# Two token groups loaded ahead of the factors, a new order of steps, and bias additions by half rows

## The chip, the cores and the metric

The kernel runs on one core of a Trainium2 chip. A core has five engines that run their own instruction streams in order: PE (TensorE, matmuls into the eight PSUM banks), DVE (VectorE), ACT (ScalarE), POOL (GpSimd) and SP (SyncE, which here issues nearly all DMAs). They wait for one another by semaphores. The metric is the device time of one launch in microseconds.

## The reference

There are 8 batches of 1024 tokens with 1024 columns, all float32, and a context of 64 rows per batch with a mask. Cut to what matters:

```python
x = x + xattn(layernorm(x), ctx, mask)       # softmax(scores / 32) times ctx, masked
h = layernorm(x)
mixed = einsum('btd,rde->bte', h, factors)   # 8 factors of 1024 x 1024, summed over r
x = x + mixed / sqrt(8) + bias
```

The sum over r can be taken first, so the second part is one product with the sum of the eight factors, scaled by 1/sqrt(8).

## The kernel before, in words

**Tiling.** The 8192 tokens are cut into 16 groups of 512. A group has four row tiles of 128 tokens, tile t = 2h + q. Two groups share one context ("memory").

**One group.** Its tokens are loaded twice: as rows (`load_rows`, L304) and, for groups from 2 on, in blocks (`load_blocks`, L293) that DVE transposes (`transpose_blocks`, L349). Groups 0 and 1 are transposed on PE (`transpose_x_pe`, L375). Then come `scores`, `scores_back`, `softmax`, `weights_back`, `read_out` (PE) and `residual` (DVE, L468, adds the attention into the rows). The first layer norm's statistics come from DVE (`row_stats`, group 0) or ACT (`row_sums`, `row_squares`). The second norm's statistics come from DVE for q = 0 (`norm_stats`, L478) and from ACT for q = 1 (`norm_sums`, `norm_squares`, L497 and L507), each followed by a few small POOL operations. `normalize` (ACT, L523) writes h. From group 1 on, h is moved by 16 DMAs of 64 KB (`relayout`, L546) and transposed by DVE (`transpose_rows`, L555); group 0 does this on PE (`transpose_h_pe`).

**The product.** h times the summed factors is done by a scheme with seven products in place of eight, for each q (`product g q p`, L585, 8 matmul instructions each). Its operand sums are made by `combine_rows` on DVE (L567). Three of the seven (p = 2, 3, 4, the list `SECOND`, L192) are split once more into seven `part g p i` (L634, 4 matmul instructions), which take both q at once, with `combine_parts` (L609). So a group has 8 `product` steps and 21 `part` steps. `give` (L601) and `give_part` (L650) add a product from PSUM, scaled, into the rows x; several products share a bank, so the next one into the bank waits for the `give` of the one before it. `add_bias` (POOL, L538) adds the bias to one row tile. `store` (L665) writes a row tile out.

**The factors.** A piece `load_factor s r` (L670) is a quarter s of the contraction of factor r, 1 MB. s = 0 and 1 fill b11 and t2, s = 2 and 3 fill b21 and b22 (named as they are held; t1, t3 and t4 are differences of these). A piece is added on DVE (`add_factor`, L676, two additions of 128x1024) or on PE through an identity matmul (`sum_factor`, L694, 8 matmul instructions). `add_sums` (L709) joins both and makes the differences; `combine_factors` (L725) makes those for the parts. `product` 1 and 5 need s = 0 and 1 alone; `product` 6 and 7 need all four quarters.

**What sets the order.** Nothing is scheduled at run time. A hand-held table `START` (L24) is run once, then `LOOP` (L76) is run for g = 0 to 16 with p = g - 1, n = g + 1, m = g + 2; a step that was already done is skipped. The order of the steps is the order of the instructions on every engine and every DMA queue. Buffers are handed out first in, first out (`Slots`, L153): 8 PSUM banks, 11 row tiles x, and 8 buffers of 8 KB per partition ("big") that factors, memory, xT, xb, h, hb and hT share. So a load waits for whatever step gave its buffer back, and everything behind it on SP's queue waits too.

Of the kernel before, what the change touches and what calls it, by code (L numbers as in the profile page):

```python
# [10 lines left out]
F32 = mybir.dt.float32  # L11
BF16 = mybir.dt.bfloat16
AF = mybir.ActivationFunctionType
ALU = mybir.AluOpType
# [10 lines left out]
load_memory 0; load_factor 0 6; add_factor 0 6; centre_memory 0; load_rows 0 0; load_bias;  # L25
constants; load_factor 0 4; load_rows 0 3; load_rows 0 2; add_factor 0 4; load_rows 0 1;
load_factor 0 7; row_stats 0 0; transpose_x_pe 0 1; load_factor 1 2; row_stats 0 1;
transpose_memory 0; load_factor 0 0; transpose_x_pe 0 0; scores 0; masks; scores_back 0;
row_stats 0 2; add_factor 1 2; row_stats 0 3; add_factor 0 0; load_factor 0 5; load_factor 0 3;
load_factor 1 0; softmax 0; load_factor 1 5; sum_factor 0 5; load_factor 2 7; weights_back 0;  # L30
read_out 0 0 0; load_factor 0 2; add_factor 1 5; load_factor 2 6; add_factor 1 0; sum_factor 0 3;
read_out 0 0 1; residual 0 0 1; residual 0 0 0; load_factor 0 1; sum_factor 0 7; add_factor 0 2;
load_factor 2 4; read_out 0 1 1; norm_stats 0 0 0; sum_factor 0 1; load_rows 1 1; add_factor 2 6;
load_rows 1 0; norm_stats 0 0 1; add_factor 2 4; normalize 0 0 0; add_sums 0 1; residual 0 1 1;
normalize 0 0 1; load_factor 1 7; load_factor 2 3; load_factor 2 5; load_factor 1 4;
transpose_h_pe 0 0 0; sum_factor 2 7; add_factor 1 7; load_factor 1 3; transpose_x_pe 1 0;
load_factor 1 6; add_sums 0 0; transpose_h_pe 0 0 1; read_out 0 1 0; add_factor 2 3;
add_bias 0 0 1; sum_factor 2 5; load_rows 1 3; load_factor 1 1; residual 0 1 0; norm_stats 0 1 0;
sum_factor 1 4; sum_factor 1 1; load_factor 2 1; load_rows 1 2; combine_rows 0 0 1;
sum_factor 2 1; norm_stats 0 1 1; add_factor 1 3; load_factor 2 2; add_factor 1 6;  # L40
load_factor 2 0; add_sums 1 1; row_sums 1 0; load_factor 3 0; add_sums 1 0; transpose_x_pe 1 1;
add_factor 2 2; add_factor 2 0; add_bias_v 0 0 0; add_sums 2 1; row_squares 1 0; load_factor 3 4;
add_factor 3 4; scores 1; add_factor 3 0; add_sums 2 0; product 0 0 1; load_factor 3 2;
normalize 0 1 0; normalize 0 1 1; transpose_h_pe 0 1 0; load_factor 3 3; add_factor 3 3;
row_sums 1 1; load_factor 3 1; load_factor 3 6; combine_rows 0 0 2; load_factor 3 7;
transpose_h_pe 0 1 1; product 0 0 5; row_squares 1 1; combine_rows 0 0 3; load_factor 3 5;
add_factor 3 2; sum_factor 3 1; combine_rows 0 0 4; scores_back 1; sum_factor 3 6; give 0 0 1;
load_rows 2 1; load_rows 2 0; add_factor 3 7; combine_rows 0 1 1; sum_factor 3 5; softmax 1;
add_sums 3 1; row_sums 2 0; product 0 1 1; weights_back 1; product 0 0 6; add_sums 3 0;
read_out 1 0 0; combine_parts 0 4 1; combine_factors 4; residual 1 0 0; read_out 1 0 1;  # L50
combine_rows 0 1 2; part 0 4 2; give 0 0 6; part 0 4 1; give_part 0 4 1; combine_parts 0 4 2;
# [54 lines left out]
def kernel(  # L106
# [17 lines left out]
    nc = tc.nc  # L124
# [28 lines left out]
    class Slots:  # L153
# [45 lines left out]
        2: ("a12", "b21", "z", True, ((0, 0),)),  # L199
        4: ("a22", "t4", "u", False, ((1, 0),)),  # L200
    }
    LAST = {"u": 7 if 4 in SECOND else 4, "v": 5 if 3 in SECOND else 3, "z": 2}
    PARTS = {
        1: ("a11", "u", True, (0, 0)),
        5: ("s1", "v", True, (1, 1)),
# [580 lines left out]
```

## Time and profile before

| what | value |
|---|---|
| time, median of 3 runs | 981.09 us (979.46 to 981.38) |
| time of the profiled execution | 981.39 us |
| its span, first to last instruction | 979.6 us |
| busy: PE | 941.1 us (96%) |
| busy: DVE | 838.6 us (86%) |
| busy: ACT | 380.8 us (39%) |
| busy: POOL | 237.9 us (24%) |
| mean granted PE clock | 0.996 |
| moved by DMA | 167.01 MB |

"Busy" is the time in which at least one instruction of the engine runs, and PE's matmuls overlap, so a PE that is 96% busy need not run at its best rate: the starts of neighbouring steps tell more. In the views, a row of the order of time has its start, its length, engine, line, operation, output and input tiles, shapes and count, and in brackets how long the engine was idle before it and what released it. "SPq" rows are DMA issues, so their length is the issuing and not the transfer.

### The profile page before, as it was taken

How to read it: one execution, taken by the hardware profiler on the slowest of the kernel's cores; microseconds unless marked ns; L12 is line 12 of the kernel's file. 1: busy time of each engine (PE TensorE's matmuls, PEld its weight loads, DVE VectorE, ACT ScalarE, POOL GpSimd, SP SyncE). 2: the span in 40 equal slices, each digit the busy share in tenths (PEclk: the TensorE clock that was granted, in tenths of full speed). 3: DMA queues.
4: the chain of work that ended last, by engine and by line, in shares of the span. 5: the costliest groups of instructions: out<-in, count | busy, mean ns of one | idle time of the engine just before them, and what ended most of it. 6: DMA issues, size and time to landing. Idle time of an engine off the chain costs nothing.

```text
span 979.6 us, 11017 instructions
## 1 busy us (share of the span) xinstructions
PE 941.1 (96%) x3456; PEld 547.0 (56%) x3456; DVE 838.6 (86%) x1510; ACT 380.8 (39%) x712; POOL 237.9 (24%) x298
## 2 busy tenths in 40 slices
PE   3889999999999999999999999999999999999998
PEld 2345455655656565655656565564656565565656
DVE  3689999979799887989799697989889788989955
ACT  3035252443616253442623455351714445252300
POOL 0021124312312232411322142321223123132300
PEclk9999999999999999999999999999999999999999
DMA  9999637475565667366465756557474746542412
GB/s 353 418 421 369 179 107 159 126 177 145 158 156 155 151 194 149 109 168 165 153 162 155 164 144 148 140 162 176 151 177 134 172 123 170 142 151 79 100 70 86
DMA packets 93530, 167.01 MB, mean 170 GB/s; under 512 B 12320, under 2 KB 71840, under 8 KB 89376
## 3 DMA queue, kind: packets, MB, share of 16 engines
q1 hardware_dynamic: 93024, 165.20, 58.4%
q10 hardware_dynamic: 448, 1.11, 0.4%
q8 instruction: 27, 0.44, 0.2%
q14 instruction: 31, 0.25, 0.1%
HBM read 101.25 MB, written 33.55 MB: 138 GB/s over the span
## 4 chain that ended last, share of the span: by engine, by line
PE 60%; DVE 26%; DMA 5%; SPq 4%; issue 3%; ACT 1%; POOL 0%; DVEq 0%; ACTq 0%; POOLq 0%
PE yu L592 24%; PE yv L592 7%; PE ro L465 5%; PE y4u L641 4%; SPq L551 4%; PE y3u L641 4%; DVE xT L356 4%; DVE x L655 3%; DVE x L605 3%; DVE hT L560 3%; PE scT L399 3%; DMA f<-in_L_ffn_factors_dram 3%; DVE hT L627 3%; PE y2u L641 2%; PE y4v L641 2%
## 5 line engine op out<-in xcount | busy, mean ns | idle before, releaser
L534 ACT ACTIVATE h<-x,nb,rstd 128x512 f32<-128x512 f32 x128 | 96.2, 822 | 211.6 <-DVE x L473 134.2
L540 POOL TENSOR_TENSOR x<-x,bias_bc 128x1024 f32<-128x1024 f32 x63 | 150.1, 2384 | 73.5 <-DVE x L605 37.7
L592 PE MATMUL yu<-b,hT 128*128 128x512 f32 x256 | 118.0, 604 | 0.0
L592 PE MATMUL yu<-t,s 128*128 128x512 f32 x256 | 115.3, 593 | 0.1
L592 PE MATMUL yv<-t,s 128*128 128x512 f32 x256 | 115.2, 593 | 0.0
L592 PE MATMUL yu<-t,hT 128*128 128x512 f32 x256 | 115.1, 592 | 0.0
L605 DVE SCALAR_TENSOR_TENSOR x<-yu,x 128x512 f32<-128x512 f32 x128 | 82.9, 675 | 19.1 <-PE yu L592 19.1
L473 DVE SCALAR_TENSOR_TENSOR x<-ro,rden,x 128x512 f32<-128x512 f32 x128 | 88.4, 741 | 3.5 <-PE ro L465 3.5
L316 ACT ACTIVATE junk<-x 128x1024 bf16<-128x1024 f32 x60 | 63.2, 1054 | 56.6 <-DMA x<-in_x_dram 55.7
L356 DVE STREAM_TRANSPOSE xT<-xb 128x256 f32<-128x256 f32 x224 | 81.6, 410 | 0.0
L592 PEld LDWEIGHTS yu<-b,hT 128*128 128x128 f32 x256 | 46.3, 189 | 62.6 <-issue 51.8
L592 PEld LDWEIGHTS yu<-t,hT 128*128 128x128 f32 x256 | 48.6, 190 | 54.4 <-issue 50.5
L592 PEld LDWEIGHTS yu<-t,s 128*128 128x128 f32 x256 | 48.4, 190 | 48.7 <-issue 45.7
L592 PEld LDWEIGHTS yv<-t,s 128*128 128x128 f32 x256 | 48.5, 190 | 48.2 <-issue 45.9
L399 PE MATMUL scT<-xT,memT 128*64 128x256 f32 x512 | 66.5, 385 | 9.2 <-DVE xT L356 9.2
L560 DVE STREAM_TRANSPOSE hT<-hb 128x1024 f32<-128x1024 f32 x60 | 73.5, 1227 | 0.7 <-issue 0.6
L328 ACT ACTIVATE junk<-x,nmean 128x1024 bf16<-128x1024 f32 x60 | 68.9, 1149 | 2.9 <-POOL nmean L317 0.7
L490 POOL TENSOR_SCALAR rstd<-mv 128x2 f32<-128x2 f32 x17 | 4.6, 269 | 253.6 <-DVE mv L487 253.6
L465 PE MATMUL ro<-mem,eT 64*128 64x512 f32 x256 | 64.5, 617 | 0.6 <-ACT eT L454 0.6
L655 DVE SCALAR_TENSOR_TENSOR x<-y3u,x 128x256 f32<-128x256 f32 x64 | 26.2, 409 | 43.9 <-PE y3u L641 43.6
L502 ACT ACTIVATE junkz<-x 128x1024 bf16<-128x1024 f32 x30 | 31.7, 1056 | 72.7 <-DVE x L473 72.2
L399 PEld LDWEIGHTS scT<-xT,memT 128*64 128x64 f32 x512 | 37.3, 136 | 36.0 <-DVE xT L356 15.0
(133 smaller groups left out, 1544.2 us busy)
## 6 DMA issues: line engine op xcount, KB each, us to landing
f<-in_L_ffn_factors_dram SPq DMA_DIRECT2D x32, 1024.0 KB, 10.8
x<-in_x_dram SPq DMA_DIRECT2D x64, 512.0 KB, 4.5
out_dram<-x SPq DMA_DIRECT2D x64, 512.0 KB, 4.4
hb<-h SPq DMA_DIRECT2D x480, 64.0 KB, 2.0
xb<-in_x_dram SPq DMA_DIRECT2D x112, 256.0 KB, 6.9
mem<-in_ctx_dram SPq DMA_DIRECT2D x14, 256.0 KB, 3.8
mem<-in_ctx_dram ACTq DMA_DIRECT2D x2, 256.0 KB, 5.8
bias_bc<-in_L_ffn_bias_dram ACTq DMA_DIRECT2D x1, 512.0 KB, 7.9
```

Source lines behind the costliest of these rows:

```text
L316: nc.scalar.activation(junk, st["x", g, t], AF.Copy, accum_out=s1[:, t : t + 1])
L328: nc.scalar.activation(junk, st["x", g, t], AF.Square, bias=nmean[:, t : t + 1], accum_out=ss[:, t : t + 1])
L356: nc.vector.transpose(xT[:, 2 * e + c].rearrange("p (t j) -> p t j", j=Q), xb.rearrange("p t (k e i c) -> p e c t k i", e=NC // 2, i=2, c= ...
L399: nc.tensor.matmul(ps[ts(h, M), : 2 * P], mT[:, c, :], st["xT", g, h][:, c, :], start=(c == 0), stop=(c == NC - 1),)
L465: nc.tensor.matmul(ps, eT[ts(h, M), q, :], m[ts(h, M), ts(n, H)], start=True, stop=True)
L473: nc.vector.scalar_tensor_tensor(xt, st.pop(("ro", g, q, n, h)), rden[:, k : k + 1], xt, ALU.mult, ALU.add)
L534: nc.scalar.activation(to, fr, AF.Identity, bias=nb[:, h : h + 1], scale=rstd[:, h : h + 1])
L540: nc.gpsimd.tensor_add(xt, xt, bias_bc)
L560: nc.vector.transpose(st["hT", g, q][:, h].rearrange("p c (t j) -> p t c j", j=Q), hb[:, h].rearrange("p t (c i) -> p t c i", i=Q),)
L592: nc.tensor.matmul(ps, lhs[:, c, :], wq[right][:, c, :], start=(first and c == 0), stop=(c == KH - 1), skip_group_check=True,)
L605: nc.vector.scalar_tensor_tensor(xt, st["y", g, q, key], ISR, xt, ALU.mult, ALU.add)
L641: nc.tensor.matmul(ps, lhs[:, c, :], wp[p][i][:, c, :], start=(first and c == 0), stop=(c == 1), skip_group_check=True,)
```

## The change

**Both tables are new.** In `START` the row tiles of groups 0 and 1 are loaded first, with only a few factor pieces between them; before, group 1's rows came after 15 to 25 pieces. Pieces are loaded by halves of the contraction: nearly all of s = 0 and 1 ahead of s = 2, and s = 3 last; before, s = 0, 1 and 2 were mixed. Group 1's attention and residual move up, in between the factor sums of s = 0 and 1. `load_bias` moves from the head of the table to behind the factor sums. One piece moves from `sum_factor` to `add_factor` (12 and 20 steps before, 11 and 21 after). `START` ends earlier in group 1: its `product` steps now begin in `LOOP`, which starts just behind `scores` of the group after next.

**Norm statistics.** `norm_stats` (DVE) is in neither table any more; all 32 row tile pairs use `norm_sums` and `norm_squares` (ACT).

**Bias.** `add_bias g q k` now adds half a row tile, k = 2h + n: 128 POOL operations of 128x512 where 63 of 128x1024 on POOL and one on DVE were.

**Loads in the loop.** Before, the four `load_rows m` stood together behind all stores of group p. Now `load_rows m 1` stands behind `store p 3`, `m 0` behind `store p 1`, `m 3` and `m 2` behind `store p 0` and `store g 2`, each ahead of a `relayout`.

**Lists.** `PRODUCTS`, `LAST` and the tag of s1 get cases for 7 and 5 in `SECOND`, and `give_part` runs over the list of places; `SECOND` itself stays (2, 3, 4).

The diff, with the tables cut to the places that the prediction names:

```diff
 START = """
-load_memory 0; load_factor 0 6; add_factor 0 6; centre_memory 0; load_rows 0 0; load_bias;
-constants; load_factor 0 4; load_rows 0 3; load_rows 0 2; add_factor 0 4; load_rows 0 1;
...
+load_memory 0; load_rows 0 2; load_rows 0 0; constants; load_rows 0 1; row_stats 0 0;
+load_rows 1 1; centre_memory 0; load_rows 0 3; load_rows 1 0; row_stats 0 1; masks;
+load_factor 1 0; load_rows 1 2; transpose_memory 0; load_factor 1 3; load_factor 1 1;
...
+load_factor 3 2; add_sums 2 0; combine_parts 0 4 1; sum_factor 3 2; load_factor 3 7; part 0 4 1;
+add_factor 3 3; load_factor 3 0; combine_parts 0 4 2; load_factor 3 5; load_factor 3 4;
+norm_squares 1 0; combine_parts 0 4 3; give 0 0 1; add_factor 3 7; load_factor 3 1;
+load_memory 2; give_part 0 4 1; sum_factor 3 6; normalize 1 0 0; load_blocks 2 0;
+normalize 1 0 1; combine_rows 0 0 4; sum_factor 3 5; give 0 1 1; add_factor 3 0; centre_memory 2;
+add_factor 3 4; add_factor 3 1; load_rows 2 0; add_sums 3 1; product 0 1 5; product 0 0 6;
...
 LOOP = """
...
-transpose_blocks m 1 3; scores m; product n 0 1; scores_back m; combine_rows n 0 1; part g 3 7;
...
+give p 1 7; transpose_rows g 0 1; give_part p 2 7; give_part p 3 6; product g 0 1; part p 3 7;
...
+transpose_rows g 1 0; combine_rows g 0 2; row_squares n 1; part p 3 4; softmax n; product g 0 6;
...
+norm_sums n 0; norm_squares n 0; load_blocks m 1; load_rows m 1; combine_parts g 4 1; part p 3 2;
...
+part g 4 2; give_part g 4 1; part g 4 6; residual n 1 0; store p 1; normalize n 0 0;
+combine_parts g 4 3; give g 1 6; part g 4 5; combine_rows g 1 3; transpose_blocks m 0 2;
+transpose_blocks m 0 3; add_bias g 0 2; combine_rows g 1 4; combine_parts g 2 1; add_bias g 1 0;
+part g 2 1; end_rows p 0; give_part g 4 2; add_bias g 0 0; give_part g 4 6; give_part g 2 1;
+product g 0 7; part g 4 7; normalize n 0 1; combine_parts g 4 4; norm_sums n 1; give_part g 4 5;
...
+combine_parts g 3 1; relayout n 0; part g 3 1; norm_squares n 1; centre_memory m; store p 0;
...
+row_sums m 0; store g 2; product g 1 7; part g 2 7; transpose_blocks m 1 3; load_rows m 3;
+scores m; give_part g 2 2; add_bias g 0 1; combine_parts g 3 4; add_bias n 1 2; part g 3 6;
+load_rows m 2; transpose_rows n 0 0; relayout n 1; part g 3 5;
 """
...
-        6: ("s2", "t2", "u", False, ((0, 1),)),
+        6: ("s2", "t2", "u", False, ((0, 1), (1, 1), (1, 0)) if 7 in SECOND else ((0, 1),)),
...
-    LAST = {"u": 7 if 4 in SECOND else 4, "v": 5 if 3 in SECOND else 3, "z": 2}
+    LAST = {"u": 6 if 7 in SECOND else 7 if 4 in SECOND else 4, "v": 5 if 3 in SECOND else 3, "z": 2}
...
-    def add_bias(g: int, q: int, h: int):
-        xt = st["x", g, 2 * h + q]
-        nc.gpsimd.tensor_add(xt, xt, bias_bc)
-
-    def add_bias_v(g: int, q: int, h: int):
-        xt = st["x", g, 2 * h + q]
-        nc.vector.tensor_add(xt, xt, bias_bc)
+    def add_bias(g: int, q: int, k: int, eng=nc.gpsimd):
+
+        xt = st["x", g, 2 * (k // 2) + q][:, ts(k % 2, H)]
+        eng.tensor_add(xt, xt, bias_bc[:, ts(k % 2, H)])
+
+    def add_bias_v(g: int, q: int, k: int):
+        add_bias(g, q, k, nc.vector)
...
-            ops["s1"] = work.tile([P, KH, P], F32, tag="s1", name=f"s1_{g}_{q}")
+            ops["s1"] = work.tile([P, KH, P], F32, tag=f"s1{q if 5 in SECOND else ''}", name=f"s1_{g}_{q}")
...
-        h, n = PRODUCTS[p][4][0]
         q, k = PARTS[i][3]
-        xt = st["x", g, 2 * h + q][:, 2 * n * HH + k * HH : 2 * n * HH + (k + 1) * HH]
-        nc.vector.scalar_tensor_tensor(
-            xt, st["yp", g, p, key][:, :HH], ISR, xt, ALU.mult, ALU.add
-        )
+        for h, n in PRODUCTS[p][4]:
+            xt = st["x", g, 2 * h + q][:, ts(2 * n + k, HH)]
+            nc.vector.scalar_tensor_tensor(
+                xt, st["yp", g, p, key][:, :HH], ISR, xt, ALU.mult, ALU.add
+            )
```

## The prediction

> **What bounds the kernel.** I read the page's slices first, then the busy time by window, then the order of time on TensorE (PE), and last the waits. The windows (busy us of each engine in each stretch, granted PE clock, DMA share, GB/s):
>
> ```profile
> core 0: us, PE busy (x) PEld busy (x) DVE busy (x) ACT busy (x) POOL busy (x), PEclk, DMA share, GB/s
> 0.00:25.00 25.00, 8.59 (x54) 7.62 (x56) 9.43 (x17) 8.66 (x13) 2.19 (x10) 1.00 0.93 353
> 25.00:50.00 25.00, 20.64 (x67) 8.70 (x64) 17.23 (x23) 3.21 (x12) 1.36 (x4) 0.93 1.01 420
> 50.00:75.00 25.00, 22.31 (x72) 11.05 (x72) 21.24 (x27) 8.60 (x15) 6.77 (x6) 0.93 1.02 421
> 75.00:100.00 25.00, 25.00 (x108) 13.39 (x106) 24.38 (x27) 14.54 (x25) 3.54 (x5) 1.00 0.93 368
> ```
>
> For 100 us the DMA engines are full: 38.8 MB (32 factor pieces, eight token tiles, memory, mask, bias) must come in. PE has gaps only here. PE in order of time, at the marks I use below:
>
> ```profile
> 16.41 3.65 PE L371 MATMUL tp<-ident,x 128*128 128x128 f32 x16 [16.41 <-DMA x<-in_x_dram]
> ...
> 100.56 3.70 PE L704 MATMUL sum<-f,ident 128*128 128x512 f32 x8 [0.40 <-DMA f<-in_L_ffn_factors_dram]
> ...
> 107.75 3.60 PE L592 MATMUL yu<-t,s 128*128 128x512 f32 x8
> ...
> 149.17 3.60 PE L592 MATMUL yu<-b,hT 128*128 128x512 f32 x8
> ```
>
> The last factor piece lands at 100.56; 107.75 is `product 0 0 6`, the first that needs all pieces; 149.17 is `product 1 0 1`. From there PE works back to back to 975.5 (826.3 us), except at the scores:
>
> ```profile
> 199.05 3.67 PE L399 MATMUL scT<-xT,memT 128*64 128x256 f32 x32
> 202.65 3.70 PE L592 MATMUL yu<-b,hT 128*128 128x512 f32 x8
> ...
> 309.40 2.37 PE L399 MATMUL scT<-xT,memT 128*64 128x256 f32 x18
> 312.57 1.94 PE L399 MATMUL scT<-xT,memT 128*64 128x256 f32 x14 [0.80 <-DVE xT L356]
> 314.44 3.70 PE L592 MATMUL yu<-b,hT 128*128 128x512 f32 x8
> ```
>
> Undisturbed scores take 3.60 us from start to the next product; with VectorE (DVE) late they take 5.04. That 1.4 us recurs in 12 groups. `product g 0 1` comes every 55.8 us (149.17 to 874.19, 13 groups); without the wait, 54.4. So a start that is limited by loads and DVE, then a PE-bound loop with one DVE wait.
>
> **Start: what the new order is worth.** PE work ahead of `product 1 0 1`, in back-to-back starts: 96 transposes 11.3, three scores 10.8, twelve `sum_factor` at 3.43 = 41.2, eight products at 3.43 = 27.5, sixteen parts at 0.86 = 13.8, eight `read_out` 7.7, small transposes 2.1: 114.4 us; the other 34.8 of 149.2 are gaps and slow matmuls. The new table puts the same set ahead of `product 1 0 1`, less one `sum_factor` (that piece goes to `add_factor` on DVE, 2.3 us there): 111.0.
>
> Loads: 8.65 MB had moved by 24.5 us and then 420 GB/s, so transfers count from 3.9 us. The three token tiles and the memory (2.1 MB) are in at about 10 us, so PE starts 6 us earlier; that alone is no gain, since PE waits for factors later. Bias (0.5 MB) leaves the load stretch; 38.3 MB end at 96 us if no buffer is late. Two are: `load_factor 3 4` takes the slot of `sum_factor 3 2` (about 90.5) and `load_factor 3 1` that of `add_factor 3 7` (about 92), so the last piece lands at 97 to 98.
>
> What decides is DVE. From `combine_rows 0 1 1` (about 77.4, after the h transposes) to `t2` ready it has five adds at 2.3 = 11.5, `add_sums` 3.7+2.5+2.5 = 8.7, gives and `give_part` 2.7, six combines 2.3: 25.2, so 102.6. I take 104.5 for `product 0 0 6`, 3.2 earlier, with both token groups' attention, `product` 1 and 5 of both row tiles and a part already done. Behind it before `product 1 0 1` stand 4 products, 15 parts, scores and a memory transpose: 13.7+13.0+3.6+0.6 = 30.9 (before: 41.4 elapsed). DVE has 22.6 us of work there until `transpose_blocks 2 1 3` against 22.9 of PE, so it gives no reserve; twelve half bias additions now run here and I charge 2.5 us for collisions. So `product 1 0 1` at 138: **gain 11**, ends 6 (DVE 2 late at 104.5 and 3 late after) and 14 (102.6 and no collision).
>
> **Loop: parts.** `norm_stats` (four BATCH_NORM_STATS2 at 680 ns and two aggregates at 209: in the queue 2.9 us a group) leaves DVE; `norm_sums` and `norm_squares` add 2.33+2.52 us to ACT, 39% busy, whose new chain for q=0 is residual, 2.3, POOL 0.3, 2.5, POOL 1.3, normalize 3.0; with the relayout behind it (10.3 of issues and 1.6) it ends some 4 us before `transpose_rows n 0 0` is due on DVE. Without that reserve, PE would wait by what is missing. Bias: 63 rows of 2384 ns become 128 halves. In proportion a half costs 1.19. [...] POOL is 24% busy; I charge nothing for its own time. What counts is the next view (order of time on POOL and DVE in one group):
>
> ```profile
> 408.76 2.46 POOL L540 TENSOR_TENSOR x<-x,bias_bc 128x1024 f32<-128x1024 f32 x1
> ...
> 408.93 2.58 DVE L627 TENSOR_TENSOR hT<-hT,hT 128x256 f32<-128x256 f32 x1
> ```
>
> The DVE row is normally 0.41; it ended with POOL's. [...] Four such hits a group cost 7.1 us here (L582 1.5, L627 2.2, L631 1.7, L431 1.7). By the row, halves cut each hit; [...] the new table puts three (`add_bias g 0 2`, `g 1 0`, `g 0 0`) in a row right where DVE is tight. That speaks against the change.
>
> **Loop: the new tight place.** With `product g 0 6` as 0, PE needs 20.6 us to the end of `part g 4 1`; `give_part g 4 1` ends at 21.1. It releases `add_bias g 0 2`, then the other two halves. PE wants `part g 4 7` at 27.6, after `give_part g 4 6`: DVE has 5.85 us ahead of it, so 26.95, reserve 0.6. In these 5.85 are four combines that the halves can block: S = 1.3 if DVE goes first, 2.6 [...]. PE's period is then 54.4 + (S - 0.6). The tile scores no longer wait: they come 8 us of DVE work later than needed.
>
> A second cycle closes over SP. The loads of tokens are now each behind a store whose row buffer they take, and `relayout n 1` is behind them:
>
> ```profile
> 471.71 0.34 SPq L666 DMA_DIRECT2D out_dram<-x  x1
> 472.10 3.03 SPq L306 DMA_DIRECT2D x<-in_x_dram  x3
> 480.35 10.54 SPq L551 DMA_DIRECT2D hb<-h  x16
> ```
>
> The third load there waited until the store landed, 3.1 us after its start; sixteen relayout issues take 10.3. New cycle: 21.1, DVE to `give_part g 4 4` 14.9 + S, store 3.1, load issue 0.5, relayout 10.3, landing 1.6, `transpose_rows g 1 0` 1.2, `combine_rows g 0 2` 0.7, hand-overs 0.2: 53.6 + S, back at `product g 0 6`. Queued behind that DVE transpose are softmax and all gives, behind the product the rest of PE. Both cycles give 55.1 to 56.5 for S from 1.3 to 2.6. I take 55.5, nearer to DVE going first, [...]: 0.27 x 13 = **gain 3.5**.
>
> **No cost.** The lists for 5 and 7 in `SECOND`, the tag of s1 and the loop in `give_part` make the same instructions with `SECOND = (2, 3, 4)`. The end keeps its form: last `give_part`, store, 4.1 us.
>
> **Sum.** 979.6 - 11 - 3.5 = 965.1 span; outside it lie 1.8 us (981.39 - 979.6), so **967 us**; the profiled run is 0.3 above the median shown.
>
> **Rivals.**
> 1. *Forecast*, 0.47: own range 957 to 976 (start 6 to 14, period 55.1 to 56.0).
> 2. *Dense loop*, 0.2: halves hardly collide, S under 0.6, period 54.4: 13 x 1.37 = 17.8 with the start, 952.6. For it: DVE loses 2.9 us a group and half a lock. Against: three halves in a row.
> 3. *SP's queue becomes the bound*, 0.15: the store lands in 4.4, as the page's median, or S is 3 or more; period 57.5, 13 x 1.7 = 22.5 lost, minus 11: 993. It decides from a period of 56.6 (0.85 x 13 = 11). For it: every load waits for a store just ahead of sixteen issues. Against: 3.1 measured with a load right behind.
> 4. *The start gives nothing*, 0.18: slot waits starve the loads or DVE is 8 us late, `product 1 0 1` at 147: 976, to 981 if the loop is as before.
>
> Within 0.2% (2 us, about what this kernel's measurement can tell) lie parts of 3 and 4: 0.06. Slower: most of 3, 0.14. Faster: 0.8. The range 950 to 984 leaves out the far end of 3 and a little below 2.
>
> **What would show it.** Start: `product 0 0 6` at 103 to 106, `product 1 0 1` at 135 to 141, its factor wait gone from PE. Loop: no wait of scT for xT; a PE gap ahead of y4u (`part g 4 7`) or ahead of `product g 0 6`, released by DVE; combines above 0.41 us beside half bias rows of 1.2 to 1.3. Wrong if `product 1 0 1` comes after 143, or if the period is under 55.0 or over 56.6.

## The result, and the profile after

The changed kernel takes **970.75 us** (median of 4, 968.06 to 973.52) where the kernel before takes 981.16 in the same comparison: ratio 0.9898, 95% interval 0.9865 to 0.993. Six more executions, taken later beside the experiments, have a median of 968.67 (966.97 to 976.93). The profiled execution took 971.97, with a span of 969.7.

First the windows of the changed kernel over the stretch that was shown of the kernel before (busy us of each engine, granted PE clock, DMA share, GB/s), with the window behind it:

```profile
0.00:25.00 25.00, 13.91 (x83) 11.39 (x84) 10.12 (x21) 12.24 (x25) 2.19 (x10) 0.94 0.95 357
25.00:50.00 25.00, 22.48 (x103) 11.72 (x101) 17.42 (x23) 18.78 (x41) 6.94 (x7) 0.93 0.91 372
50.00:75.00 25.00, 22.84 (x72) 10.98 (x73) 24.41 (x30) 18.12 (x32) 6.60 (x9) 1.00 0.99 394
75.00:100.00 25.00, 25.00 (x68) 11.93 (x67) 23.36 (x28) 6.48 (x10) 2.85 (x4) 1.00 0.98 384
100.00:125.00 25.00, 20.81 (x63) 11.17 (x63) 21.39 (x32) 5.47 (x9) 3.02 (x4) 0.93 0.89 187
```

PE does 5.3 us more in the first window than before and starts at 8.03 in place of 16.41. But the loads run at 372 and 394 GB/s where they ran at 420 and 421, so less had come in by 75 us. What this does to PE's marks stands in its order of time:

```profile
104.54 1.88 PE L588 MATMUL yu<-t,s 128*128 128x512 f32 x4
110.61 3.62 PE L588 MATMUL yu<-t,s 128*128 128x512 f32 x4 [4.19 <-DVE t L716]
...
134.37 3.67 PE L395 MATMUL scT<-xT,memT 128*64 128x256 f32 x32
...
141.63 1.13 PE L637 MATMUL y3u<-b,r 128*128 128x256 f32 x4 [0.80 <-DVE x L651]
142.60 1.03 PE L637 MATMUL y2u<-tau,hT 128*128 128x256 f32 x4
143.47 2.74 PE L588 MATMUL yu<-b,hT 128*128 128x512 f32 x6
```

`product 0 0 6` begins at 104.54 with its first half of the contraction and stands 4.19 us for t2 before the second half. `product 1 0 1` comes at 143.47, against 149.17: the start gives **5.7 us**. From there to the end it is 969.7 - 143.47 = 826.2 us against 830.4: the loop gives **4.2**. In the loop, scores no longer wait, and one gap stands in their place (PE's order of time, two stretches):

```profile
303.44 3.67 PE L395 MATMUL scT<-xT,memT 128*64 128x256 f32 x32
307.04 1.13 PE L637 MATMUL y3u<-b,r 128*128 128x256 f32 x4
...
399.48 3.60 PE L588 MATMUL yu<-t,hT 128*128 128x512 f32 x8
404.04 1.13 PE L637 MATMUL y4u<-tau,hT 128*128 128x256 f32 x4 [0.96 <-DVE x L651]
```

The second gap is the one at `part g 4 7` and comes in every group. It is the only wait of PE that the view of waits shows between the scores at 192.32 and those at 859.07 (us in total, times, longest):

```profile
PE y4u L637 <- DVE x L651: 11.5, 12, 1.0
```

These scores are 12 groups apart, so the period is **55.56 us**; by the same measure the kernel before has 55.84. DVE in the same place, then POOL (order of time):

```profile
396.23 0.42 DVE L651 SCALAR_TENSOR_TENSOR x<-y4u,x 128x256 f32<-128x256 f32 x1 [4.05 <-PE y4u L637]
...
398.82 1.18 DVE L574 TENSOR_TENSOR hT<-hT 128x512 f32<-128x512 f32 x1
...
401.83 1.49 DVE L617 TENSOR_TENSOR r<-hT 128x256 f32<-128x256 f32 x1
...
403.57 0.41 DVE L651 SCALAR_TENSOR_TENSOR x<-y4u,x 128x256 f32<-128x256 f32 x1
```

```profile
396.73 4.39 POOL L537 TENSOR_TENSOR x<-x,bias_bc 128x512 f32<-128x512 f32 x3 [1.60 <-DVE x L651]
401.10 0.21 POOL L500 TENSOR_SCALAR zm<-zs 128x2 f32<-128x2 f32 x1
401.27 1.76 POOL L537 TENSOR_TENSOR x<-x,bias_bc 128x512 f32<-128x512 f32 x1
```

The first DVE row is `give_part g 4 1`, the last `give_part g 4 6`. Between them two combines are long: L574 by 0.5 us (normally 0.68) and L617 by 1.08 (normally 0.41). Their sum is the prediction's S, here 1.58. The first lies beside the three halves that the prediction named. The longer one lies beside a **fourth** half, at 401.27: `add_bias n 0 3`, which stands further down in the table, and which POOL reaches this early because it waits for nothing there. So DVE and POOL hold each other up: the combine takes 1.49 in place of 0.41, and the half beside it 1.76, where the one at 393.86, with DVE idle, takes 1.28. This is called the lock from here on.

### The profile page after: what moved, and what is told of

Its sections match the earlier page's. It is cut to its first block, busy times and chain, and to the rows that moved or that the text cites. A ratio compares the mean times of both kernels' runs of the same rounds, so it can differ in the third digit from the quotient of the medians.

```text
span 969.7 us, 11176 instructions
## 1 busy us (share of the span) xinstructions
PE 930.3 (96%) x3448; PEld 548.4 (57%) x3448; DVE 734.7 (76%) x1409; ACT 462.4 (48%) x848; POOL 280.3 (29%) x363
## 4 chain that ended last, share of the span: by engine, by line
PE 71%; DVE 19%; DMA 6%; issue 1%; ACT 1%; POOL 1%; SPq 1%; DVEq 0%
PE yu L588 26%; PE yv L588 10%; PE y3u L637 6%; PE scT L395 5%; DVE x L469 5%; PE y4u L637 5%; PE y2u L637 4%; DMA out_dram<-x 3%; PE y3v L637 3%; PE y2v L637 3%; DMA f<-in_L_ffn_factors_dram 2%; DVE xT L352 2%; DVE r L617 2%; PE ro L461 2%; DVE x L651 2%; PE y3z L637 2%
## 5 line engine op out<-in xcount | busy, mean ns | idle before, releaser
L537 POOL TENSOR_TENSOR x<-x,bias_bc 128x512 f32<-128x512 f32 x128 | 187.6, 1482 | 84.0 <-DVE x L651 70.3
L588 PE MATMUL yu<-b,hT 128*128 128x512 f32 x256 | 114.9, 592 | 0.0
L498 ACT ACTIVATE junkz<-x 128x1024 bf16<-128x1024 f32 x64 | 67.6, 1057 | 66.3 <-DVE x L469 65.3
L509 ACT ACTIVATE junky<-x,zm 128x1024 bf16<-128x1024 f32 x64 | 73.6, 1149 | 28.5 <-POOL zm L500 27.4
L500 POOL TENSOR_SCALAR zm<-zs 128x2 f32<-128x2 f32 x32 | 11.1, 348 | 259.5 <-ACT junkz L498 259.5
L556 DVE STREAM_TRANSPOSE hT<-hb 128x1024 f32<-128x1024 f32 x60 | 74.0, 1233 | 10.3 <-DMA hb<-h 10.3
L588 PEld LDWEIGHTS yu<-b,hT 128*128 128x128 f32 x256 | 48.6, 190 | 54.8 <-issue 54.0
L651 DVE SCALAR_TENSOR_TENSOR x<-y4u,x 128x256 f32<-128x256 f32 x64 | 26.5, 415 | 63.2 <-PE y4u L637 63.2
L461 PE MATMUL ro<-mem,eT 64*128 64x512 f32 x256 | 62.0, 613 | 0.8 <-ACT eT L450 0.6
L313 POOL TENSOR_SCALAR nmean<-sum 128x2 f32<-128x2 f32 x30 | 10.9, 362 | 178.9 <-ACT junk L312 178.9
```

What stands on the lines that cost most here:

```text
L461: nc.tensor.matmul(ps, eT[ts(h, M), q, :], m[ts(h, M), ts(n, H)], start=True, stop=True)
L498: nc.scalar.activation(junk, st["x", g, 2 * h + q], AF.Copy, accum_out=s1[:, h : h + 1])
L509: nc.scalar.activation(junk, st["x", g, 2 * h + q], AF.Square, bias=nmean[:, h : h + 1], accum_out=ss[:, h : h + 1])
L537: eng.tensor_add(xt, xt, bias_bc[:, ts(k % 2, H)])
L556: nc.vector.transpose(st["hT", g, q][:, h].rearrange("p c (t j) -> p t c j", j=Q), hb[:, h].rearrange("p t (c i) -> p t c i", i=Q),)
L588: nc.tensor.matmul(ps, lhs[:, c, :], wq[right][:, c, :], start=(first and c == 0), stop=(c == KH - 1), skip_group_check=True,)
```

## The experiments

Each was compared with the kernel before on its own chip, and its median stands here with the ratio to that and the 95% interval. "Period" is from the scores of the profiled execution, 12 groups apart; "t2" is the start of the second half of `product 0 0 6`, "p101" that of `product 1 0 1`. These three come from one profiled execution each, which in three kernels (the same again; fourth half later; two factor additions with the fourth half later) is the slowest of its own.

| kernel | median, us | ratio to before | period | t2 | p101 |
|---|---|---|---|---|---|
| changed kernel | 970.75 | 0.9898 (0.9865 to 0.993) | 55.56 | 110.61 | 143.47 |
| the same again | 968.67 | 0.9888 (0.9861 to 0.9915) | 55.56 | 107.47 | 147.01 |
| fourth half later | 955.54 | 0.9755 (0.9726 to 0.9784) | 54.48 | 107.26 | 145.07 |
| three halves later | 957.28 | 0.9772 (0.9744 to 0.98) | 54.49 | 108.32 | 140.47 |
| all four later | 958.65 | 0.9777 (0.9753 to 0.9801) | 54.34 | 105.85 | 143.51 |
| whole bias rows in LOOP | 975.08 | 0.9951 (0.9935 to 0.9967) | 55.94 | 106.92 | 141.59 |
| norm_stats back on DVE | 975.24 | 0.9945 (0.9928 to 0.9961) | 55.56 | 108.25 | 147.75 |
| new START, old LOOP | 978.60 | 0.9978 (0.996 to 0.9995) | 55.92 | 106.11 | 138.36 |
| softmax gap filled | 973.19 | 0.993 (0.991 to 0.995) | 55.56 | 110.64 | 143.48 |
| four later, gap filled, b22 first | 959.82 | 0.9799 (0.9775 to 0.9822) | 54.34 | 109.34 | 143.25 |
| two factor additions earlier | 972.65 | 0.9904 (0.9869 to 0.9939) | 55.56 | 105.98 | 143.71 |
| the same, and fourth half later | 951.93 | 0.9713 (0.9697 to 0.9729) | 54.48 | 107.63 | 140.70 |
| the same, and START's halves moved | 956.95 | 0.977 (0.9749 to 0.9791) | 54.48 | 106.17 | 142.64 |

### The loop: which half makes the gap

The fourth half moved alone:

```diff
-transpose_blocks m 1 0; give_part g 2 6; part g 2 2; add_bias n 0 3; end_rows p 1; give g 0 7;
+transpose_blocks m 1 0; give_part g 2 6; part g 2 2; end_rows p 1; give g 0 7;
...
-scores m; give_part g 2 2; add_bias g 0 1; combine_parts g 3 4; add_bias n 1 2; part g 3 6;
+scores m; give_part g 2 2; add_bias g 0 1; add_bias n 0 3; combine_parts g 3 4; add_bias n 1 2;
```

> Only `add_bias n 0 3` moves in LOOP, from behind `part g 2 2` to behind `add_bias g 0 1`. In the changed kernel this half ran from 401.27 to 403.03 in the group looked at, and `combine_parts g 2 1` stood from 401.83 to 403.32 beside it, some 1.08 us over its 0.41; PE's gap ahead of `part g 4 7` was 0.95. Theory A (the fourth half, which the prediction did not count, makes the gap): the combine falls back to 0.4, the gap goes, the period goes from 55.56 to 54.5 to 54.8 (12 to 13 groups by 0.8 to 1.05), time 957 to 962. Theory B (the three halves of the prediction make it): the combine loses its stall only to the third of the three or to the hand-over, the gap stays at 0.7 or more, period 55.3 to 55.6, time 968 to 972.

The three halves moved alone, and below it all four moved:

```diff
-transpose_blocks m 0 3; add_bias g 0 2; combine_rows g 1 4; combine_parts g 2 1; add_bias g 1 0;
-part g 2 1; end_rows p 0; give_part g 4 2; add_bias g 0 0; give_part g 4 6; give_part g 2 1;
+transpose_blocks m 0 3; combine_rows g 1 4; combine_parts g 2 1; part g 2 1; end_rows p 0;
+give_part g 4 2; give_part g 4 6; give_part g 2 1;
...
-give_part g 4 3; transpose_blocks m 1 1;
+give_part g 4 3; add_bias g 0 2; add_bias g 1 0; add_bias g 0 0; transpose_blocks m 1 1;
```

> Only the three halves `add_bias g 0 2`, `g 1 0`, `g 0 0` move behind `give_part g 4 3`; `add_bias n 0 3` stays. Moving the fourth half alone has already closed PE's gap at `part g 4 7`. Theory A (the three push the fourth into the place: they hold POOL from 396.7 to 401.1, and the fourth waits behind them and the small POOL operation zm): without them the fourth runs at about 399.9 to 401.2, ahead of `combine_rows g 1 4` at 401.26, the combines have no stall above 0.2, the gap is below 0.3, the period 54.4 to 54.7, time 955 to 960. Rival (the fourth is enough by itself: it starts when zm and ACT's normalize let it, which is late in any case): a combine is still stalled by 0.8 to 1.1, the gap is 0.4 to 0.7, the period 54.8 to 55.2, time 962 to 967.

> The three halves `add_bias g 0 2`, `g 1 0`, `g 0 0` move behind `give_part g 4 3`, and `add_bias n 0 3` behind `add_bias g 0 1`; nothing of POOL's bias work is then between `give_part g 4 1` and `give_part g 4 6`. Theory A (lock collisions there are the whole of the gap): S falls from about 1.6 to 0, PE has no gap at `part g 4 7`, the period is that of the dense loop, 54.4 to 54.6, and the time 971 - 13 x 1.0 to 1.15 = 956 to 958, since the second cycle over SP (relayout) has about 1.5 us of reserve. Rival (the second cycle becomes the bound: the halves now fall on combines ahead of `give_part g 4 4` and `store g 2`, and DVE's transposes wait longer for the relayout): a gap moves to `product g 0 6` or to the scores, period 55.0 to 55.6, time 964 to 971.

Theory A held in all three for what it says of the gap: PE has no wait at `part g 4 7`, and the period is 54.34 to 54.49. The times were less exact (955.54 against 957 to 962, 958.65 against 956 to 958); single times spread over 5 to 9 us, so the three medians give no order. With the fourth half moved, PE's order of time, DVE's and POOL's at the same place read:

```profile
396.91 3.60 PE L588 MATMUL yu<-t,hT 128*128 128x512 f32 x8
400.38 1.13 PE L637 MATMUL y4u<-tau,hT 128*128 128x256 f32 x4
```

```profile
396.25 1.17 DVE L574 TENSOR_TENSOR hT<-hT 128x512 f32<-128x512 f32 x1
...
399.25 0.41 DVE L617 TENSOR_TENSOR r<-hT 128x256 f32<-128x256 f32 x1
```

```profile
394.16 4.38 POOL L537 TENSOR_TENSOR x<-x,bias_bc 128x512 f32<-128x512 f32 x3 [1.61 <-DVE x L651]
398.51 0.21 POOL L500 TENSOR_SCALAR zm<-zs 128x2 f32<-128x2 f32 x1
```

The three halves still cost L574 its 0.5 us, but L617 is back at 0.41 and PE goes on without a gap. With the three moved instead, the fourth ran at 393.34, earlier than the 399.9 that was expected, cost one combine (L578) 0.42, and the gap was gone as well. So neither alone makes it: the three halves push the fourth onto the combine, and the sum passes the reserve. PE's gap follows S less the 0.6 us of reserve in the prediction: S = 1.58 gave 0.96, S = 0.5 and 0.43 gave none. (From start to start PE loses 1.09, 4.56 us from 399.48 to 404.04 against 3.47 from 396.91 to 400.38, since steps without a gap overlap a little; this is the 1.08 of the period.) One moved step of POOL is worth 13 to 15 us by the two medians of the changed kernel; the period alone gives 13 x 1.08 = 14.

**Whole rows.** In LOOP the bias is added by whole row tiles (`add_row`, 128x1024), each in the place of its later half:

```diff
-transpose_blocks m 0 3; add_bias g 0 2; combine_rows g 1 4; combine_parts g 2 1; add_bias g 1 0;
-part g 2 1; end_rows p 0; give_part g 4 2; add_bias g 0 0; give_part g 4 6; give_part g 2 1;
+transpose_blocks m 0 3; add_row g 0 1; combine_rows g 1 4; combine_parts g 2 1; add_row g 1 0;
+part g 2 1; end_rows p 0; give_part g 4 2; give_part g 4 6; give_part g 2 1;
```

> In LOOP the bias is added by whole row tiles again (128x1024), each in the place of the later of its two halves; START keeps its halves. In the tight place stand then two rows (tile 2 and tile 1) in place of three halves, and the fourth half goes to the place of `add_bias g 0 2`. Theory A (the split into halves pays: a DVE combine waits for the end of the whole POOL instruction): one or two combines wait up to 2.4 each, S 2.5 to 4, period 56.3 to 57.8, time 980 to 1000. Theory B (what counts is how long POOL holds the place, and that is 4.8 us by rows against 4.4 and 1.8 by halves): S 1 to 1.8, period 54.9 to 55.7, time 962 to 973.

The period of 55.94 and S (1.9, below) lie between the two theories. DVE, POOL and PE in its order of time (lines there are up to 10 higher):

```profile
396.45 1.49 DVE L633 TENSOR_TENSOR hT<-hT,hT 128x256 f32<-128x256 f32 x1
...
400.40 1.51 DVE L588 TENSOR_TENSOR hT<-hT,s 128x512 f32<-128x512 f32 x1
```

```profile
395.29 2.37 POOL L544 TENSOR_TENSOR x<-x,bias_bc 128x1024 f32<-128x1024 f32 x1 [0.50 <-DVE x L661]
398.62 2.74 POOL L544 TENSOR_TENSOR x<-x,bias_bc 128x1024 f32<-128x1024 f32 x1 [0.96 <-DVE x L611]
```

```profile
402.96 1.13 PE L647 MATMUL y4u<-tau,hT 128*128 128x256 f32 x4 [1.33 <-DVE x L661]
```

Each of the two rows hits one combine, by 1.07 and 0.83, S = 1.9, and the gap is 1.33: 1.9 - 0.6 again. A hit costs about what is left of POOL's instruction when DVE asks (1.21 and 0.96 us here), and not its length. The rows come out 0.38 us a group behind the changed kernel, some 5 us in all, and not at twice its collisions. But this compares two placings as much as two sizes: the fourth half has gone into the first row, and `add_bias g 0 0` has left the place. Against halves with the fourth one moved (54.48) the rows cost 1.46. And 55.94 is no better than the 55.84 of the kernel before: with rows in these places, the new order alone gains nothing in the loop, since the lock takes back what the scores no longer wait.

**norm_stats back on DVE**, which undoes that part of the change in LOOP:

```diff
-norm_sums n 0; norm_squares n 0; load_blocks m 1; load_rows m 1; combine_parts g 4 1; part p 3 2;
+norm_stats n 0 0; norm_stats n 0 1; load_blocks m 1; load_rows m 1; combine_parts g 4 1; part p 3 2;
```

> In LOOP, `norm_sums n 0; norm_squares n 0` (ACT) become `norm_stats n 0 0; norm_stats n 0 1` (DVE, some 2.9 us a group) in the same place. Theory A (DVE's total is not what the new loop hangs on: DVE waits 4.05 us for PE just ahead of `give_part g 4 1`, and the statistics fit in there): period 55.4 to 55.7, time 968 to 973, DVE busy some 50 us higher. Rival (the prediction's reason: DVE has to lose these 2.9 us for the tight place to hold): `give_part g 4 1` and all behind it come 1 to 2.9 later, the gap ahead of `part g 4 7` grows from 0.95 to 2 to 3.8, period 56.6 to 58.4, time 985 to 1008.

The period stayed at 55.56, with DVE busy for 779.5 us in place of 734.7. The two rows that decide it, DVE and PE:

```profile
401.65 0.42 DVE L652 SCALAR_TENSOR_TENSOR x<-y4u,x 128x256 f32<-128x256 f32 x1 [1.26 <-PE y4u L638]
```

```profile
409.45 1.13 PE L638 MATMUL y4u<-tau,hT 128*128 128x256 f32 x4 [0.96 <-DVE x L652]
```

DVE's wait for PE ahead of `give_part g 4 1` fell from 4.05 to 1.26, so the 2.8 us went into a wait, and PE's gap is as it was. The median of 975.24 is above the expected 968 to 973; its one profile has 4.3 us of that in the start (p101 at 147.75), whose table is the same.

### The start: why 5.7 and not 11

**The tables apart.** The new START, unchanged, with the old LOOP (whose bias steps are whole rows):

```diff
 LOOP = """
-give p 1 7; transpose_rows g 0 1; give_part p 2 7; give_part p 3 6; product g 0 1; part p 3 7;
...
+load_blocks m 0; row_squares n 1; give g 0 1; part p 2 3; give_part p 2 4; softmax n; part p 3 2;
...
```

> The new START with the old LOOP (norm_stats on DVE, whole bias rows, loads of tokens together). Theory A (the two tables' gains add): the start gives the 5.7 us by which `product 1 0 1` came earlier, the old period of 55.8 stays, time 981.2 - 5.7 = 975 to 976. Rival 1 (the start's gain is only kept because the new loop takes up group 1 where the new start leaves it): the first rounds of the old loop stall, the time is 979 to 985. Rival 2 (the loop's gain is really the start's, the old loop runs dense once it is entered otherwise): period under 55.2, time under 970.

The median of 978.60 lies just below rival 1's range and misses theory A's. With the old LOOP the new START is worth 2.3 us at the median, but the single times run from 972.33 to 986.08 (20 executions, granted clock 0.998 to 0.991), while those of the kernel before lie within 978.91 and 982.15. Neither theory had this spread. The profiled execution took 973.86, among the five fastest of the 20. In it `product 1 0 1` came at 138.36, as predicted; the old LOOP then took 833.4 us from there, 3.0 more than in its own kernel. So rival 1 holds in part: PE waits 0.85 and 1.07 us for DVE soon behind `product 1 0 1`, where the kernel before has no wait, and the period is 0.08 longer.

**The same kernel again** (no edit):

> The changed kernel once more, beside the next two on one chip, to see how much its start varies. Theory A (the start varies with PE's granted clock): the period is 55.56 and unchanged, PE's gap of 0.95 ahead of `part g 4 7` is there in each group, while `product 0 0 6` and `product 1 0 1` differ from 110.6 and 143.5 by up to 5 us with the clock of the first 150 us, and the single times spread over 5 us or more, where those of the kernel before spread over 3. Rival (the first profile shows the start as it always is): `product 1 0 1` within 1 us of 143.5 and times within 2 us of each other.

Theory A's figures held: t2 3.1 us earlier, p101 3.5 later, times spread over 10 us. That the clock is the cause is not shown by this: most of the later p101 belongs to the lock (the stretch behind t2, below). Behind p101 the two profiles take 826.2 and 827.7 us, so the start makes the spread; if the loop takes as long in the others, their spans of 964.7 to 974.7 us put p101 between about 137 and 147 (an estimate). The start's gain then runs from 2 to 12 us, and 5.7 is one draw of it.

The clock in its windows from 100 to 150 is 0.86, in slices of 3 us down to 0.50 from 108 to 117, behind the 3.99 us in which PE stood for t2, and again from 141 to 150. What lowers it the traces do not settle. In the changed kernel the clock is 0.50 from 24 to 27 us, and no single wait of PE between its first instruction at 8.03 and that stretch is above 2.31 us, with short transposes in between. In three kernels (fourth half later, all four later, two factor additions earlier) it halves between 138 and 147 us with no single wait over 1.1 us in the 10 us ahead. With the new START and the old LOOP PE stood 2.96 us for t2, and the clock stayed at 1.00 behind that. What does come out is the length: taken as half rate, each stretch of lowered clock up to 159 us in the fourteen profiles lasts 3.4, 6.8 or 10.3 us (twice the share that is missing in slices of 3 us), which is once, twice or three times the shortest.

**Does the clock hold back the loads?** Loads wait for the buffers that `scores 1` gives back. In the view of waits of SP, from 12.5 to 37.5 us, changed kernel:

```profile
SPq L670 <- PE scT L395: 15.9, 2, 9.4
```

Two kernels: one fills PE's gap at the softmax, the other takes the next two loads off PE:

```diff
-softmax 0; load_factor 1 7; load_rows 1 3; row_sums 1 0; weights_back 0; transpose_x_pe 1 0;
+softmax 0; load_factor 1 7; load_rows 1 3; transpose_x_pe 1 0; weights_back 0; row_sums 1 0;
```

> Only START changes: `transpose_x_pe 1 0` (16 transposes on PE, 3.6 us) moves ahead of `weights_back 0`, into the time in which PE has nothing but two small transposes while group 0's softmax runs (19.5 to 23.3), and `row_sums 1 0` behind it. Theory A (the clock: PE's granted clock falls to a half for some 6 us after that idle time, PE loses 3.4 us, `scores 1` gives its buffers back later, and the factor stream stands): the clock is 1.00 from 12.5 to 37.5, the DMA rate from 25 to 37.5 us is 390 to 420 GB/s instead of 341, the first addition behind the last piece starts at 98 to 101 instead of 105.5, `product 0 0 6` goes on at 105 to 106 instead of 110.6, and the median time is 2 to 4 below 970.75, with the loop's period at 55.56 as it is. Rival (the last piece is late for its own slot, given back by DVE and PE at 90 to 95, whatever the clock does at 20 to 30): `product 0 0 6` stays at 108 to 111, time 969 to 972.

It missed, with 973.19 us and t2 at 110.64. The gap moved: PE stood 1.96 us for eT, whose copy now stands behind four others in ACT's order, and the clock from 25 to 37.5 was 0.87. As the clock did not rise, this tests nothing of what it does. The second kernel:

```diff
+add_factor 1 1; add_factor 1 7;
 residual 0 0 1; row_squares 1 0; read_out 0 1 1; residual 0 1 1; transpose_x_pe 1 1;
...
-add_factor 1 2; add_factor 1 1; norm_sums 0 0; add_factor 1 7; load_factor 0 6; load_factor 2 3;
+add_factor 1 2; norm_sums 0 0; load_factor 0 6; load_factor 2 3;
```

> Only START changes: `add_factor 1 1` and `add_factor 1 7` (DVE, 2.3 us each) move ahead of `residual 0 0 1`, where DVE stood 3.26 us for PE. Their two buffers then come back ahead of those of `scores 1`, so the third and fourth next factor loads hang on DVE and not on PE's scores. Theory A (the factor stream stands because its loads wait for `scores 1`, and stands longer the lower PE's clock is at 20 to 35): the DMA rate from 25 to 37.5 us is 405 to 420 GB/s instead of 341 to 393, the last piece's addition starts at 98 to 101, `product 0 0 6` goes on at 103 to 106, the median is 2 to 5 below that of the changed kernel on the same chip. Rival (a later slot wait takes up the gain, or DVE is behind by then): the rate from 25 to 37.5 rises, the last addition does not come before 101 and the time is within 1 us of the changed kernel.

Theory A held as far as t2: 422 GB/s from 25 to 37.5 us, the last addition at 100.91, t2 at 105.98. It failed for the time, 972.65 in place of 2 to 5 us below 968.67; the rival's "within 1 us" failed too. In the profile the gain goes behind t2, in a stretch of 37.7 us (below).

The same START, with `add_bias n 0 3` moved in LOOP as above:

> The last kernel's START together with `add_bias n 0 3` behind `add_bias g 0 1` in LOOP. Theory A (the two gains add): the gap at `part g 4 7` is gone, period 54.5, and the start's gain of 2 to 5 is kept: 951 to 954 against 955.5 for the moved half alone. Rival (in the denser loop DVE, not the factors, limits the first two groups): 955 to 958, `product 1 0 1` not before 140.

The time of 951.93 and the period of 54.48 are theory A's.

The windows from 12.5 to 37.5 us, first of the changed kernel, then of the last of these two, which happened to have the same clock:

```profile
12.50:25.00 12.50, 9.50 (x62) 7.39 (x61) 5.85 (x13) 6.68 (x18) 1.23 (x2) 0.87 1.02 420
25.00:37.50 12.50, 12.00 (x75) 7.80 (x75) 8.93 (x11) 9.83 (x20) 2.95 (x4) 0.86 0.83 341
```

```profile
12.50:25.00 12.50, 9.50 (x62) 7.39 (x61) 5.79 (x13) 6.66 (x18) 1.23 (x2) 0.87 1.02 419
25.00:37.50 12.50, 12.00 (x75) 7.82 (x75) 11.54 (x13) 10.58 (x21) 2.02 (x4) 0.85 1.03 424
```

With the same clock and the same PE work, 341 GB/s became 424, and t2 came at 107.63 in place of 110.61. The three kernels with the two additions moved have 422 to 424 at clocks from 0.85 to 1.00. The ten profiles with the old coupling have 392 and 393 with the clock at 1.00 in both windows (12.5 to 25 and 25 to 37.5 us), 355 to 387 in between, and 341 and 345 where its mean over the two was lowest. So the chain "lower clock, later `scores 1`, later buffers, later loads" is shown for the loads. For t2 it is worth about 3 us: in the three profiles at 341 to 355 GB/s t2 came at 109.3 to 110.6, in the seven at 366 to 393 at 105.9 to 108.3, with the additions moved at 106.0 to 107.6. Whether it reaches the end is not shown: alone, the second kernel's median lies 4 us above that of the changed kernel on the same chip (times 964.43 to 976.82), together with the moved half it is 3.6 lower than that half alone, on another chip, and the intervals of the two ratios (0.9697 to 0.9729 and 0.9726 to 0.9784) just touch.

**What lies between t2 and p101.** This stretch takes 32.1 to 33.9 us in six of the twelve profiles that share START's bias steps, 37.7 to 39.5 in five, 34.7 in one. DVE and POOL in an execution of the second kind (the changed kernel again):

```profile
120.24 0.72 DVE L725 TENSOR_TENSOR b<-b,tau 128x512 f32<-128x512 f32 x1
120.99 1.64 DVE L726 TENSOR_TENSOR tau<-b 128x512 f32<-128x512 f32 x1
122.56 1.75 DVE L727 TENSOR_TENSOR tau<-b 128x512 f32<-128x512 f32 x1
124.23 1.48 DVE L621 TENSOR_TENSOR r<-r,hT 128x256 f32<-128x256 f32 x1
```

```profile
120.37 5.06 POOL L537 TENSOR_TENSOR x<-x,bias_bc 128x512 f32<-128x512 f32 x3
```

The three halves take 5.06, where three of 1.27 make 3.8, and each of the last three DVE operations pays about 1.0 (0.42 to 0.69 without POOL). Five to seven pay so in all, here and at `combine_factors 3`. In the first kind no such operation there takes over 1.4. The last kernel moves three of START's halves away:

```diff
-part 0 2 5; add_bias 0 1 2; give_part 0 4 3;
+part 0 2 5; give_part 0 4 3;
...
-part 0 4 4; add_bias 0 1 3; part 0 3 1; load_rows 2 3; normalize 1 1 1; add_bias 0 0 0; row_sums 2 0;
+part 0 4 4; part 0 3 1; load_rows 2 3; normalize 1 1 1; row_sums 2 0;
...
 give_part 0 2 5; give_part 0 4 4;
+add_bias 0 1 2; add_bias 0 1 3; add_bias 0 0 0;
```

> The last kernel (two factor additions ahead of `residual 0 0 1`, `add_bias n 0 3` behind `add_bias g 0 1`), and in START `add_bias 0 1 2`, `0 1 3` and `0 0 0` moved behind `give_part 0 4 4`. Runs with the same START fall into two kinds so far: from `product 0 0 6` to `product 1 0 1` PE takes 32 to 35 us where no long stall is seen, and 37.7 to 39.5 where POOL has started a row of three halves just ahead of `combine_factors 2`, and three DVE operations there and two at `combine_factors 3` take 1.5 to 1.75 each in place of 0.42 to 0.69 (some 5 us). Theory A (which kind comes is the lock, and the moved halves are its cause): no operation of both `combine_factors` takes over 1.4, the stretch is 31.5 to 33.5, `product 1 0 1` comes at 137 to 140, the times spread over 4 us or less, median 949 to 952. Rival (the moved halves collide with the combines behind `give_part 0 4 4` and with `combine_rows 1 0 1` instead, or hold POOL's small operations for the softmax of group 2): the stretch is the same but the first groups of the loop lose 1 to 3 us, time 952 to 956.

It missed. One operation of `combine_factors` still took 1.64, the stretch was 36.5 us in place of 31.5 to 33.5, p101 came at 142.64, and a new wait came in its place (DVE's order of time):

```profile
140.33 0.42 DVE L650 SCALAR_TENSOR_TENSOR x<-y3u,x 128x256 f32<-128x256 f32 x1 [3.69 <-POOL x L536]
```

`give_part 0 3 1` adds into the same half tile as `add_bias 0 0 0`, which now stood ahead of it in a queue of eight halves; PE waited 2.3 us for it. The median is 956.95, slower than without the move (ratios 0.977 and 0.9713): a dependence was made where only a lock had been. Which small difference decides between the two kinds stays open.

**b22 first.** Four halves later, gap filled, and in `add_factor 3 1` the addition for b22 first, with `add_sums 3 1` between the two:

```diff
-add_factor 3 4; add_factor 3 1; load_rows 2 0; add_sums 3 1; product 0 1 5; product 0 0 6;
+add_factor 3 4; add_factor 3 1 1; load_rows 2 0; add_sums 3 1; add_factor 3 1 0; product 0 1 5;
+product 0 0 6;
```

> All four halves moved away from the tight place, the transposes in START moved into the softmax gap, and the last factor piece added by halves: b22's addition, `add_sums 3 1` (b22, t2, t3), then b21's, so t2 comes one addition of 128x1024 (1.15 us) sooner. Theory A (the start's gains arrive at the end): 958.65 less 1.15 less 1 to 3 for the clock, 953 to 956. Rival (behind `product 0 0 6` DVE is the bound of the start, as PE's wait of 2.3 us for a give ahead of `product 0 1 7` in the kernel with the four halves moved says): the time stays at 957 to 959.

959.82: no gain over the four halves alone (958.65), with the clock at 0.75 from 25 to 37.5 and t2 at 109.34. The step itself did what it should: t2 came 3.94 us behind the start of the last piece's addition (105.40), where it is 5.07 in the other kernels. In the time nothing is seen of this, since the start varies by more than the 1.15 us in question.

**The best version** is the kernel with the two factor additions and the fourth half moved: 951.93 us, 0.9713 of the kernel before (0.9697 to 0.9729). The changed kernel had 968.67 beside it on the same chip, 1.8% more.

## Why the prediction was right, and where a term was off

- **Time and bound of each part.** 967 was forecast, 970.75 measured. The two gains were 11 and 3.5 in the sum; the profiled execution has 5.7 and 4.2. So the time was near, but the start gave half of what was forecast there, and the loop met its figure by another cause than the one named.
- **Loop: right in place, form and size, the size by luck.** The gap came ahead of `part g 4 7`, released by DVE, at S - 0.6; period 55.56 against 55.5. In the two kernels in which S and a gap were read the reserve is 0.62 and 0.57, and S up to 0.5 left no gap. But the forecast charged the three halves with 1.3 to 2.6 (the author's estimate for one half or two), and they cost 0.5, which is less than the reserve: by its own sum there would have been no gap, and the period would have been that of the second rival (54.48 with the fourth half moved). S came to 1.58 only because `add_bias n 0 3`, which the prediction did not count because it stands further down in the table, cost 1.08. A queue that holds nothing back brings a later step forward: its place in the table is a bound from one side only.
- **norm_stats off DVE.** The 2.9 us were counted as DVE's relief and as evidence for the dense loop. Undone, they change no period: in the new order DVE waits for PE in that place. The new LOOP's gain comes from scores that stand later and no longer wait, and it lasts only as far as the lock leaves it (whole rows: 55.94).
- **Half rows.** 1.2 to 1.3 was forecast, 1.19 in proportion, and the upper end was an estimate of the author's; a half alone takes 1.27 to 1.28, twice that is 2.55 against 2.37 for a row, so the split costs 0.18 us a row. The mean over the run is higher (1.48 us), since a half beside a long DVE combine takes longer, as the 1.76 at 401.27 above:

```profile
L537 POOL TENSOR_TENSOR x<-x,bias_bc 128x512 f32<-128x512 f32 x128 | 187.6, 1482 | 84.0 <-DVE x L651 70.3
```

- **Three halves in a row** spoke against the change in the prediction. The row does not shut DVE out: in the changed kernel L574 ends at 400.00, while the halves beside it run from 396.73 to 401.12. But where DVE has several operations lined up beside such a row, three of them pay nearly one half each (1.0 us of 1.27, in START).
- **Start: the failed term** is "the last piece lands at 97 to 98", and with it "DVE decides". DVE was idle for the last two pieces (DVE's order of time, changed kernel):

```profile
101.26 2.36 DVE L685 TENSOR_TENSOR b<-b,f 128x1024 f32<-128x1024 f32 x2 [1.85 <-DMA f<-in_L_ffn_factors_dram]
...
105.54 2.36 DVE L685 TENSOR_TENSOR b<-b,f 128x1024 f32<-128x1024 f32 x2 [1.92 <-DMA f<-in_L_ffn_factors_dram]
```

  The last one was in at about 105.5, 7 to 8 us late, and t2 followed at 110.6 in place of 104.5. In all profiles of the new START the addition of the last piece waits for it and begins at 100.8 to 105.6, and t2 comes 5.07 us behind (3.94 with b22 first). So the loads decide, and DVE does not. The view of the DMAs for the issue of the last piece (KB, us to landing), changed kernel, then the kernel before:

```profile
f<-in_L_ffn_factors_dram SPq DMA_DIRECT2D x1, 1024.0 KB, 9.8
```

```profile
f<-in_L_ffn_factors_dram SPq DMA_DIRECT2D x1, 1024.0 KB, 5.5
```

  Slot and landing share the delay. The slot was forecast for 92; SP issued the piece at 95.6, and at 91.5 to 95.4 in the other profiles. The forecast left 5 to 6 us for the landing, as in the kernel before; it took 9.8. So some 3.6 us of the lateness are the slot's and some 4 the landing's.

  For the slot: waits were seen only for the last two pieces; those at 25 to 37 us, behind `scores 1`, were missed, and a full clock was taken for granted, although PE had now been put on the loads' path.

  For the landing: from 96 to 105.5 us the DMA engines were 98% busy and moved 290 GB/s, in the kernel before 413 from 95 to 100.5. What slows it was not tested; `load_memory 2` and the first blocks of group 2 are issued right behind the piece here, in the kernel before two rows and then blocks. The landing stays long where the slot is in time: 92.8 to 102.5 in the best version. With the clock at 1.00 from 25 to 37.5 us, t2 came at 105.85 in one kernel and 108.25 in another.

  The second part of the start was right for the profiled execution: 33.5 from t2 to p101 by the forecast, 32.9 measured; its 2.5 us for collisions lie between two kinds that are 5 us apart. Two small slips of the sums don't matter: its figures put the end of the loads at 95.1 (3.9 + 38.3 / 0.42) and not 96, and both cycles of the loop at 55.1 to 56.4 and not 56.5.
- **Rivals.** The SP cycle was no bound: DVE waits 1.29 us for hb ahead of `transpose_rows g 1 0`, but `product g 0 6` keeps 1.5 us of reserve, and with all four halves moved the period falls to 54.34 with SP's order unchanged. The dense loop of the second rival exists, but needs a half moved. The fourth rival's start (`product 1 0 1` at 147, 976 us) is that of the second profile of the changed kernel: 147.01, 976.93 us.
- **The point at which it would be wrong** (p101 after 143) was passed by 0.5 us in the first profile and by 4 in the second, and 5.7 lies just outside the forecast's 6 to 14 for the start. That the time still came close to 967 is owed to the loop, whose gain was met by luck, and to the width of the range.

## What to carry to other kernels

Where two engines hold each other up, as DVE's combine (1.49 us in place of 0.41) and POOL's half (1.76 in place of 1.27) did, look up in the trace when the other engine really runs each of its instructions, not where they stand in the program: `add_bias n 0 3`, which waited for nothing, ran at 401.27, well ahead of its place in the table, and moving it was worth 13 to 15 us, more than the whole change (10.4). Compare the sum of the stalls in one tight place with the reserve there: below the reserve of 0.6 us they cost nothing here (0.5), above it (1.58) PE lost 1.08 us in every round. And when work is pulled forward in a start that lives on loads, ask which buffers it gives back, since its own waits then become the loads': with loads that hung on `scores 1` the rate from 25 to 37.5 us was 341 GB/s, and 424 at the same PE work (clock 0.86 and 0.85) once two of them no longer did.

## What was not expected of the hardware

- The changed kernel's start takes either of two courses, with the same instructions: 32.9 us from t2 to p101 in one execution and 39.5 in the other. In the slow one seven DVE operations take 1.4 to 1.75 us beside POOL's bias halves (0.42 to 0.69 without them).
- PE's granted clock halves for 3.4, 6.8 or 10.3 us, mostly behind stands of 2 to 5.4 us, in some cases with none over 1.1 us just ahead. The kernel before has such dips as well (0.86 from 37.5 to 50 and from 62.5 to 75 us), with 419 GB/s in both windows, so its loads lose nothing; its times spread over 3 us, those of the new START over up to 14.
